# Cross-attention steps that go on in every cell, an earlier norm, and one unit's softmax sums by products with ones

## The chip, the cores and the metric

The kernel runs on one core of one Trainium2 chip. The metric is the device time of one execution in microseconds (us). The kernel before was run three times: 1612.68, 1615.26 and 1616.85 us, median 1615.26. The profiled execution is a fourth one. All arithmetic is in 32-bit floats. In this document PE is the matmul engine (TensorE), PEld its weight loads, DVE is VectorE, ACT is ScalarE, POOL is GpSimd and SP is SyncE.

## The reference

Two transformer blocks run one after the other on x, 2 sequences of 1024 tokens of width 256, with 16 heads of width 16. Each block is self-attention, cross-attention to 64 context rows, and a feed-forward part:

```
x = x + MHA_self(LN(x))                      # 1024 keys per sequence
x = x + MHA_cross(LN(x), context)            # 64 keys per sequence
    s = q @ k.T / 4  (block 2: + mask * -10000)
    a = exp(s - max(s)) / sum(exp(s - max(s)));  out = (a @ v) @ Wo
block 1:  h = LN(x); two of eight experts per token (top-2 of h @ Wr);
          x = x + sum of gate_e * (gelu(h @ W1_e) @ W2_e)
block 2:  x = x + gelu(LN(x) @ W1) @ W2
```

## The kernel before, in words

**Order of work.** Engines execute their queues in the order in which the Python program issues instructions, and that order is written by hand. The program walks over *cells*. A block has 128 of them (`ncell`): 16 groups (2 sequences, 2 halves of queries, 4 groups of four heads) of 8 key blocks. A cell issues, for four heads at once, four score products "b" with the keys on the output partitions (L817), their exponentials (ACT, L823, four to a cell), and for the cell that lies LEAD = 10 ahead four score products "a" (L806) whose row maxima DVE reduces (L813). Every second cell adds the products with the values (L868), copied by ACT (L880 or L877) and added by POOL (L881). Cells 0 to 117 have "a" work (`has_a`); cells 118 to 127 have "b" alone. I call the latter the ten last cells. `maxima[0]` is true where `has_a` is.

**The side work.** Everything else is a generator (a task) in a `Stream`: keys, queries and values of later heads, projections, the cross-attention, and in block 1 the routing ("dispatch"), the search for expert tiles ("find") and the expert slots. A step is what a generator issues until it yields. A yield above zero is a planner's estimate of its PE time. A yield of zero or less holds the task back for at least one cell, more for -3.4 or the like (CELL = 2.9). Each cell adds `max(pace, ...)` to a budget `owed` and calls `stream.step` while it lasts; `pace` is at least RATE = 2.5 us in block 1 and 1.1 us in block 2. In even cells the value product comes first, and if `owed` is below 2.5 the cell ends there with `continue`. At 2.5 per cell this never stops block 1, while in block 2 it does in most even cells. Among the tasks that are able, one with a due time (`last`) goes first, then the one of highest rank. After the last cell, `Stream.rest` issues what is left by rank alone.

**The cross-attention chain.** Each block has four units of 512 tokens, n = 0 to 3 (`cross_tasks`). A unit becomes known when its self-attention output has been projected: `project` (called at cells 39, 71 and 103 for n = 0, 1, 2, and after the cells for n = 3) calls `when_ready`. A unit has three tasks: `norm`, `weigh`, `share`. `norm` waits for the unit before to be weighed. `weigh` makes Q (L1114), then scores (SC, L1148, copied by ACT at L1159), the mask by POOL in block 2 (MA, L1178), the maximum by DVE and its subtraction by POOL (LA, L1168 and L1169), and then goes one of two ways:

- *whole*, if `maxima[0]` is true when it starts: exponentials on ACT (EX, L1185), sums and reciprocals on DVE (L1191, L1192), the division by POOL or DVE (DI, L1193), transposes (TU, L1201, ACT copy L1206) and the value product (PR, L1215). Its steps are laid out in 19 cells (21 in block 2).
- *not whole*: transposes first, exponential on the way out of PSUM (L1208), then `undivided` (value product L1230, sums by products with columns of ones L1240, reciprocal on DVE L1249), and `division` (reciprocals spread by a product, L1255, multiplied by DVE, L1262).

`share` projects the result (L438) and adds it to x (L446). Scores that are made while `maxima[0]` is false get block 2's mask by products with ones on PE (L1139) and their maximum and subtraction by DVE. In the run before, units 0, 1 and 2 of block 1 and 0 and 1 of block 2 are whole; unit 3 of block 1 and units 2 and 3 of block 2 are not.

**What follows a unit.** In block 1, `dispatch_task(n)` waits for `share(n)`, then `find` and `rows`; expert slot 0 needs units 0 and 1, slots 1 to 4 need unit 2, the others unit 3. In block 2, `forward_norm` and `forward_task` follow.

Of the kernel before, what the change touches and what calls it, by code (L numbers as in the profile page):

```python
# [121 lines left out]
class Task:  # L122

    def __init__(self, steps, cost, first=-99, last=None, mark=None, after=(), rank=0):
        self.steps, self.left, self.first = steps, cost, first
        self.soft, self.last = last is None, 9999 if last is None else last
        self.mark, self.after, self.rank = mark, after, rank


class Stream:
# [20 lines left out]
    def step(self, cell):  # L153
        while True:
            able = [t for t in self.tasks if t.first <= cell and self.made.issuperset(t.after)]
            if not able:
                return None
            cost = self.advance(min(able, key=lambda t: (t.last, -t.rank)), cell)
            if cost and cost > 0.0:
                return cost  # L160

    def pace(self, cell):

# [39 lines left out]
def two_blocks(  # L203
# [323 lines left out]
    def self_attention(layer, tail, heads, arrive, extra, when_ready, beside=None):  # L527
# [432 lines left out]
        for cell in range(ncell + 2):  # L960
            now[0] = cell
            ahead = cell + LEAD
            if ahead < ncell and ahead % 16 == 0:
                need_heads(ahead // 8)
            has_a, has_b = ahead < ncell, cell < ncell
            maxima[0] = has_a
            a = [("a", ahead, j) for j in (2, 3, 0, 1)] if has_a else []
            s = [("b", cell, j) for j in range(4)] if has_b else []
            if has_a:
                slot(s[:2] + a[:2])  # L970
                slot(s[2:] + a[2:])
            elif has_b:
                slot(s)
            if ahead % 8 == 7 and has_a:
                h = ahead // 8
                collect(h)
                stream.add(largest(h), 0.75, first=cell + 1, last=cell + 2, mark=("QB", h))
            if (cell + 1) % 8 == 0 and cell + 1 < ncell:
                stream.until(("QB", (cell + 1) // 8))
            for go in later.pop(cell, []):  # L980
                go()
            owed = min(owed, 3.0) + max(stream.pace(cell), 0.0 if has_a else 2.0)
            if cell >= 2 and cell % 2 == 0:
                product([c for c in (cell - 2, cell - 1) if c not in alone])
                if owed < 2.5:
                    continue
            most = 3.0
            while owed > 0.6 and most > 0.0:
                cost = stream.step(cell)
                if cost is None:  # L990
                    break
                owed -= cost
                most -= cost

            if cell % 2 == 1 and most > 2.0 and cell < ncell:
                alone.add(cell - 1)
                product([cell - 1])
# [79 lines left out]
    def cross_tasks(stream, layer, n, pool, first):  # L1077


        att = 2 * layer + 1  # L1080
        w = weights[att]
        b, t0 = n // 2, 4 * n
        name = f"c{layer}{n}"
        held = {}
# [14 lines left out]
        stream.add(  # L1099
            share(w, name, t0, held), 5.0, mark=("cross", n),  # L1100
            after=[("weighed", n)], rank=50,
        )

    def weigh(layer, b, pool, w, name, held):

        att = 2 * layer + 1
        kbd, vbd = kbds[layer], vbds[layer]
# [3 lines left out]
        for g in range(2):  # L1111
            i, p = bank()
            for k in range(2):
                nc.tensor.matmul(  # L1114
                    p,
                    lhsT=w[:, X_Q + k * D + g * P : X_Q + k * D + (g + 1) * P],
                    rhs=xT[:, k, :],
                    start=(k == 0),
                    stop=(k == 1),
                )  # L1120
            nc.scalar.activation(
                q[:, g, :], p, AF.Identity, bias=cols[:, C_Q[att] + g : C_Q[att] + g + 1]
            )
# [149 lines left out]
        if whole:  # L1273

            m = layer
            cells = [[] for _ in range(19 + 2 * m)]
            for k in range(8):
                g, r = divmod(k, 4)
                at = k + (4 + m) * g
                if r % 2 == 0:  # L1280
                    cells[at].append((SC, g, r // 2))
                    cells[at + 7 + m].append((TU, g, r // 2))
                if m:
                    cells[at].append((MA, g, r))
                cells[at + m].append((LA, g, r))
                cells[at + m + 2].append((EX, g, r))
                cells[at + m + 3].append((DI, g, r))
            for g in range(2):
                cells[11 + m + (7 + m) * g].append((PR, g))
            for now in cells:  # L1290
                for step, *args in now:
                    step(*args)
                us = sum(costs.get(step, 0.0) for step, *_ in now)
                if us:
                    yield us
                if now is not cells[-1]:
                    yield 0.0 if maxima[0] else -1.5
            return
        for step, *args, wait in (
            (SC, 0, 0, None),  # L1300
            (SC, 0, 1, -1.0),
# [15 lines left out]
    def share(w, name, first, held):  # L1317

        if held["division"]:
            yield -2.6  # L1320
            held["division"](1)
            yield 0.55
        yield -1.2
        for t0 in range(0, 4, 2):
            yield from project_task(held["ot"], w, first + t0, t0, 2)


    inside = const.tile([P, E], F32, name="inside")
# [869 lines left out]
```

## Time and profile before

| what | us |
|---|---|
| median of three runs | 1615.26 |
| the profiled execution | 1614.59 |
| its span, first to last instruction | 1612.8 |
| cells 0 to 117 of block 1, about | 53.5 to 536 |
| its ten last cells, about | 536 to 566 |
| the rest of block 1, and the experts, about | 566 to 951 |
| cells 0 to 117 of block 2, about | 951 to 1404 |
| its ten last cells, about | 1404 to 1431 |
| the rest of block 2, about | 1431 to 1612.8 |

The span is the time between the first and the last instruction; 1.79 us of the profiled execution lie outside it. The stages are read off from the starts of the exponentials of L823, four to a cell. In a stretch of cells with no side work at all (cells 25 to 27 of block 1) these starts lie 2.92 us apart; with side work a cell takes 3 to 8 us. In the ten last cells they lie 2.4 us apart where nothing else is done.

Where the unit steps ran in the cells before (from the starts of their lines):

| unit | Q (L1114) | first scores | projected (L438) |
|---|---|---|---|
| block 1, n=0 | cell 51 | 52 | 71 to 73 |
| block 1, n=1 | 80 | 81 | 101 to 103 |
| block 1, n=2 | 112 | 113 | 583.7 to 587.3 us, in the rest |
| block 1, n=3 | in the rest | 602.8 us | 639 to 643 us |
| block 2, n=0 | 55 | 61 | 88, 89 |
| block 2, n=1 | 97 | 99 | 123 |
| block 2, n=2 | in the rest | 1444.9 us | 1476.9 us |

### The profile page before, as it was taken

The numbers are of one execution on the slowest core, as the hardware profiler recorded it, in microseconds if no ns is written. First come the engines' busy times: TensorE is split into PE (matmuls) and PEld (weight loads), VectorE is DVE, ScalarE is ACT, GpSimd is POOL, SyncE is SP. The second block draws the span as 40 slices with busy tenths as digits, with TensorE's granted clock in tenths as the row PEclk, the third lists the DMA queues.
The fourth block names the chain that finished last, engine by engine and source line by source line (L and its number), as shares of the span: only waits on it lengthen the run. The fifth ranks groups of instructions, "written<-read, shape, count | busy, mean of one in ns | idle before, by whom it ended". The sixth has DMA issues, their size and how long they took to land. (4 is left out here: it accounts for less than half of the span.)

```text
span 1612.8 us, 27523 instructions
## 1 busy us (share of the span) xinstructions
PE 1560.5 (97%) x10182; PEld 853.7 (53%) x10182; DVE 1013.8 (63%) x2178; ACT 939.3 (58%) x1821; POOL 472.2 (29%) x589
## 2 busy tenths in 40 slices
PE   7999999999999888899999999999999999999998
PEld 3533443443444356688888753344344444446766
DVE  5788776877878856511114458876777878845400
ACT  3488777866867752332333337876777877864321
POOL 2234333433623302311112032411333525511000
PEclk9899999998999999999999999999999999999999
DMA  5236211100100214475656321101110001000000
GB/s 157 113 134 226 81 34 29 34 14 21 41 25 18 67 49 134 153 272 189 203 190 234 92 73 28 35 21 22 34 34 21 22 27 70 22 28 1 14 13 26
DMA packets 55749, 120.98 MB, mean 75 GB/s; under 512 B 12218, under 2 KB 26428, under 8 KB 55228
## 3 DMA queue, kind: packets, MB, share of 16 engines
q1 hardware_dynamic: 51772, 109.02, 21.0%
q0 software_dynamic: 3456, 9.51, 1.6%
q8 instruction: 82, 1.34, 0.3%
q10 hardware_dynamic: 384, 0.66, 0.2%
q14 instruction: 55, 0.45, 0.1%
HBM read 71.64 MB, written 38.88 MB: 69 GB/s over the span
## 5 line engine op out<-in xcount | busy, mean ns | idle before, releaser
L813 DVE TENSOR_REDUCE mx_s<-banks 128x1 f32<-128x512 f32 x1024 | 633.2, 680 | 187.0 <-PE banks L806 182.5
L823 ACT ACTIVATE pt_s<-banks 128x512 f32<-128x512 f32 x1024 | 532.9, 611 | 134.8 <-PE banks L806 107.0
L806 PE MATMUL banks<-KS,QS 16*128 16x512 f32 x2048 | 535.0, 631 | 0.2 <-issue 0.2
L817 PE MATMUL banks<-qb_s,KS 32*128 32x512 f32 x2048 | 516.5, 624 | 7.2 <-DVE qb_s L716 2.3
L881 POOL TENSOR_TENSOR acc_s<-acc_s,part_s 128x512 f32<-128x512 f32 x151 | 191.6, 1269 | 370.3 <-ACT part_s L880 369.2
L817 PEld LDWEIGHTS banks<-qb_s,KS 32*128 32x128 f32 x2048 | 179.3, 187 | 194.5 <-DVE mx_s L813 116.3
L868 PE MATMUL banks<-pt_s,v_s 128*20 128x512 f32 x2048 | 265.8, 604 | 2.6 <-DVE mx_s L813 1.9
L806 PEld LDWEIGHTS banks<-KS,QS 16*128 16x128 f32 x2048 | 199.1, 185 | 64.9 <-issue 29.5
L1731 PE MATMUL banks<-w_slot,h_s 128*128 128x256 f32 x640 | 145.2, 384 | 0.0
L868 PEld LDWEIGHTS banks<-pt_s,v_s 128*20 128x20 f32 x2048 | 42.4, 98 | 191.7 <-ACT pt_s L823 142.9
L1731 PEld LDWEIGHTS banks<-w_slot,h_s 128*128 128x128 f32 x640 | 121.7, 192 | 20.4 <-DVE mx_s L813 1.5
L1740 DVE SCALAR_TENSOR_TENSOR ys<-banks,gate,b 128x256 f32<-128x256 f32 x40 | 19.3, 483 | 172.0 <-PE banks L1731 167.7
L880 ACT COPY part_s<-banks 128x512 f32<-128x512 f32 x166 | 100.3, 605 | 45.8 <-PE banks L868 41.3
L1746 POOL DMA_INDIRECT results<-ys,to x40 | 38.7, 967 | 261.5 <-DVE ys L1740 183.2
L1707 ACT ACTIVATE h_s<-banks,w_slot 128x256 f32<-128x256 f32 x104 | 43.6, 470 | 111.3 <-issue 64.0
L1701 PE MATMUL banks<-xsT,w_slot 128*128 128x256 f32 x416 | 96.2, 383 | 0.9 <-ACT xsT L377 0.9
L1701 PEld LDWEIGHTS banks<-xsT,w_slot 128*128 128x128 f32 x416 | 78.0, 191 | 15.4 <-DVE mx_s L813 2.3
L636 PE MATMUL banks<-xT_s,w_att 128*128 128x512 f32 x128 | 63.9, 635 | 0.5 <-DVE mx_s L813 0.5
L1864 ACT ACTIVATE h_f<-banks,w_ff 128x512 f32<-128x512 f32 x32 | 22.0, 687 | 69.7 <-PE banks L1861 69.7
L1873 PE MATMUL banks<-w_ff,h_f 128*128 128x256 f32 x256 | 57.3, 380 | 0.0
L1707 ACT ACTIVATE h_s<-banks,spare 128x256 f32<-128x256 f32 x56 | 23.5, 470 | 57.3 <-issue 33.4
L1861 PE MATMUL banks<-hT_f,w_ff 128*128 128x512 f32 x128 | 56.8, 594 | 0.0
(282 smaller groups left out, 1666.0 us busy)
## 6 DMA issues: line engine op xcount, KB each, us to landing
w_slot<-in_ff_w_dram SPq DMA_DIRECT2D x40, 576.0 KB
sorted_rows<-fill SPq DMA_DIRECT2D x36, 520.0 KB
w_slot<-in_ff_w_dram SPq DMA_DIRECT2D x26, 514.0 KB
whole<-acc_s SPq DMA_DIRECT2D x30, 256.0 KB
spare<-in_ff_w_dram SPq DMA_DIRECT2D x14, 514.0 KB
xs<-sorted_rows SPq DMA_DIRECT2D x20, 260.0 KB
y<-results SPq DMA_DIRECT2D x16, 256.0 KB
QS<-stq_s SPq DMA_DIRECT2D x124, 32.0 KB
```

What stands on the lines that cost most here:

```text
L636: nc.tensor.matmul(p, lhsT=w[:, at + k * D + pair * P : at + k * D + (pair + 1) * P], rhs=xT[b][:, k, blk * 512 : (blk + 1) * 512], start= ...
L806: nc.tensor.matmul(sc, lhsT=QS[h % 4][r, qc * P : (qc + 1) * P], rhs=K[r, kh * 512 : (kh + 1) * 512], start=True, stop=True,)
L813: return i, lambda: nc.vector.tensor_reduce(mx[h][:, qc, j, kh : kh + 1], sc, AX.X, ALU.max)
L817: nc.tensor.matmul(sc, lhsT=K[r, n * P : (n + 1) * P], rhs=QB[h][r, :], start=True, stop=True)
L823: nc.scalar.activation(pt, sc, AF.Exp, scale=SCALE)
L868: nc.tensor.matmul(o[32 * j : 32 * j + VW, :], lhsT=V[b][:, cell % 8, 4 * g + j, :], rhs=exps.pop((cell, j)), start=(cell == cells[0]), st ...
L880: nc.scalar.copy(part, o)
L881: helper().tensor_tensor(acc[h], acc[h], part, ALU.add)
L1701: nc.tensor.matmul(ph[:, n, :], lhsT=w[:, at : at + P], rhs=xT[:, k, :], start=(k == 0), stop=(k == 1),)
L1707: nc.scalar.activation(h1[:, f, :], ph[:, n, :], AF.Gelu, bias=w[:, W_B1 + f : W_B1 + f + 1])
L1731: nc.tensor.matmul(py, lhsT=h1[:, f, h * P : (h + 1) * P], rhs=w[:, f * D : (f + 1) * D], start=(f == 0), stop=(f == 7),)
L1873: nc.tensor.matmul(py[:, n, :], lhsT=h1[:, f, t * P : (t + 1) * P], rhs=w2[:, f * D : (f + 1) * D], start=(f == 0), stop=(f == 7),)
```

## The change

1. Tasks can be `steady`. In every cell with "a" work a new call `go_on` runs each steady task whose marks are made and whose hold is over, again and again until it has to wait for the next cell. It is called in the even cells too, ahead of `continue`. What it issued is taken from the budget afterwards. The steady tasks are `project`'s, and `norm`, `weigh` and `share` of each unit.
2. `norm` of a unit waits for Q of the unit before (mark `asked`), not for its weights. `weigh` still waits for the unit before to be projected.
3. Unit 2 of block 1 is not whole, even though it starts while `maxima[0]` is true. For that there is a new order of steps, one cell each.
4. `project` and `share` get a `yield 0.0` between their two halves, so that with `go_on` these fall into two cells.

```diff
@@ class Stream
+    def go_on(self, cell):
+        total = 0.0
+        for t in [t for t in self.tasks if t.steady]:
+            while t in self.tasks and t.first <= cell and self.made.issuperset(t.after):
+                total += max(0.0, self.advance(t, cell) or 0.0)
+        return total
@@ project (and share alike)
                 for t0 in range(0, 4, 2):
                     yield from project_task(ot[b, qh], w, b * TB + 4 * qh + t0, t0, 2)
+                    if t0 == 0:
+                        yield 0.0
...
-            stream.add(go(), 4.0, last=now[0] + 4, rank=60, after=after)
+            stream.add(go(), 4.0, last=now[0] + 4, rank=60, after=after, steady=True)
@@ the loop over cells
                 if owed < 2.5:
+                    if has_a:
+                        owed -= stream.go_on(cell)
                     continue
             most = 3.0
+            going = stream.go_on(cell) if has_a else 0.0
+            owed -= going
+            most -= going
             while owed > 0.6 and most > 0.0:
@@ cross_tasks
-        before = [(m, n - 1) for m in ("cross", "weighed")] if n > 0 else ["context"]
-        stream.add(norm(), 2.0, mark=("cnorm", n), after=before[1:], first=first,
-            rank=67 if layer == 0 else 40)
+        before = ("cross", n - 1) if n > 0 else "context"
         stream.add(
-            weigh(layer, b, pool, w, name, held), 17.0,
-            mark=("weighed", n), after=[("cnorm", n), before[0]], rank=30,
+            norm(), 2.0, mark=("cnorm", n), after=[("asked", n - 1)] if n > 0 else [], first=first,
+            rank=67 if layer == 0 else 40, steady=True,
+        )
+        stream.add(
+            weigh(layer, b, pool, w, name, held, lambda: stream.made.add(("asked", n))), 17.0,
+            mark=("weighed", n), after=[("cnorm", n), before], rank=30,
+            steady=True,
         )
@@ weigh
+        asked()
...
-        whole = maxima[0]
+        whole = maxima[0] and (layer, b, held["half"]) != (0, 1, 0)
...
+        if maxima[0]:
+            for now, wait in (
+                (((SC, 0, 0), (LA, 0, 0)), 0.0),
+                (((LA, 0, 1),), 0.0),
+                (((SC, 0, 1), (LA, 0, 2)), 0.0),
+                (((TU, 0, 0), (LA, 0, 3)), 0.0),
+                (((SC, 1, 0), (LA, 1, 0)), 0.0),
+                (((TU, 0, 1), (LA, 1, 1)), 0.0),
+                (((SC, 1, 1), (LA, 1, 2)), 0.0),
+                (((undivided, 0), (LA, 1, 3)), -1.5),
+                (((TU, 1, 0),), None),
+                (((division, 0), (TU, 1, 1)), -1.4),
+                (((undivided, 1),), None),
+            ):
+                for step, *args in now:
+                    step(*args)
+                us = sum(costs.get(step, 0.0) for step, *_ in now)
+                if us:
+                    yield us
+                if maxima[0]:
+                    yield 0.0
+                elif wait is not None:
+                    yield wait
+            return
```

More of the change, by code (lines that the diff above doesn't have):

```diff
@@ L122, with __init__ @@
 class Task:
-    def __init__(self, steps, cost, first=-99, last=None, mark=None, after=(), rank=0):
-        self.steps, self.left, self.first = steps, cost, first
+    def __init__(
+        self, steps, cost, first=-99, last=None, mark=None, after=(), rank=0, steady=False
+    ):
+        self.steps, self.left, self.first, self.steady = steps, cost, first, steady
         self.soft, self.last = last is None, 9999 if last is None else last
@@ L1083, in cross_tasks @@
         name = f"c{layer}{n}"
-        held = {}
+        held = {"half": n % 2}
         def norm():
@@ L1100, in cross_tasks, with weigh @@
             share(w, name, t0, held), 5.0, mark=("cross", n),
-            after=[("weighed", n)], rank=50,
+            after=[("weighed", n)], rank=50, steady=True,
         )
-    def weigh(layer, b, pool, w, name, held):
+    def weigh(layer, b, pool, w, name, held, asked):
         att = 2 * layer + 1
@@ L1298, in weigh @@
             return
+        if maxima[0]:
[11 more added lines that the diff above has]
+                (((undivided, 1),), None),
+            ):
+                for step, *args in now:
[8 more added lines that the diff above has]
+            return
         for step, *args, wait in (
@@ L1325, in share @@
             yield from project_task(held["ot"], w, first + t0, t0, 2)
+            if t0 == 0:
+                yield 0.0
     inside = const.tile([P, E], F32, name="inside")
```

## The prediction

> **What bounds the kernel now.** I read the page's busy time first, then its slices, then a table of stages, then what PE waits for where it idles.
>
> ```profile
> PE 1560.5 (97%) x10182; PEld 853.7 (53%) x10182; DVE 1013.8 (63%) x2178; ACT 939.3 (58%) x1821; POOL 472.2 (29%) x589
> ...
> PE   7999999999999888899999999999999999999998
> ...
> PEclk9899999998999999999999999999999999999999
> ```
>
> PE is the bound nearly everywhere; it misses 52 us of the span. Slices 14 to 17 of 40, about 525 to 685 us, are the one broad hole: the end of block 1's cells and the chain after them. The stages, with busy us of PE, PEld, DVE, ACT and POOL and the granted clock:
>
> ```profile
> 463.00:536.00 73.00, 70.51 (x503) 31.20 (x505) 63.31 (x136) 48.47 (x95) 28.35 (x49) 0.97 0.08 27
> 536.00:566.00 30.00, 27.77 (x212) 10.46 (x204) 22.72 (x60) 26.75 (x54) 5.09 (x5) 0.96 0.16 54
> 1404.00:1431.00 27.00, 26.52 (x199) 10.33 (x196) 12.34 (x38) 23.36 (x48) 2.73 (x2) 1.00 0.03 11
> 566.00:600.00 34.00, 27.74 (x152) 19.15 (x153) 22.52 (x74) 15.67 (x32) 3.16 (x3) 1.00 0.17 59
> 600.00:643.00 43.00, 37.22 (x275) 26.88 (x274) 24.63 (x84) 12.04 (x24) 9.70 (x10) 0.92 0.34 112
> 643.00:690.00 47.00, 40.25 (x187) 33.23 (x186) 26.80 (x120) 17.99 (x35) 18.64 (x21) 0.93 0.50 172
> ```
>
> From 463 to 536 (cells with "a") PE is full and DVE is at 87%. In the ten last cells of either block (536 to 566, 1404 to 1431) ACT is the fullest after PE, at 87 to 89%, and PE's own work there is less than its busy time says: one cell's "b" products take 1.14 us and its share of the value products 0.96 us by the timeline, 21 us for ten, while the cells last 27 to 30. PE waits inside these for exponentials. From 566 to 690 PE idles 18.8 us:
>
> ```profile
> PE banks L370 <- DVE xd_m L1364: 6.5, 1, 6.5
> PE banks L370 <- DVE xn_c L358: 3.6, 2, 1.9
> PE banks L1240 <- issue: 3.1, 6, 1.1
> PE banks L370 <- DMA ctx<-in_ctx_dram: 2.2, 1, 2.2
> PE banks L1437 <- DVE chosen_m L1417: 1.2, 1, 1.2
> PE banks L1201 <- DVE sc_c L1169: 0.9, 2, 0.7
> ```
>
> Columns: us in total, times, longest. Most of it is DVE being late in a normalization or in the routing, with PE's queue standing behind a transpose. These are latencies that the planner's fixed holds did not cover, so having more expert slots at hand does not by itself remove them.
>
> The rows that price the change (busy us, mean ns | idle before):
>
> ```profile
> L1178 POOL TENSOR_TENSOR sc_c<-sc_c,mask_i 128x512 f32<-128x512 f32 x16 | 20.0, 1275 | 13.6 <-ACT sc_c L1159 13.6
> ...
> L1240 PE MATMUL banks<-pt_c,picks 128*32 128x128 f32 x192 | 8.3, 280 | 3.1 <-issue 3.1
> ```
>
> L1178 x16 says that two units of block 2 are whole now. L1240 x192 is six calls of `undivided`, two per unit that is not whole.
>
> **What the skill says.** The Trainium skill, "Perfetto Trace Analysis", Identifying the Most-Contended Engine, says that matmul busy time is a poor measure because matmuls are pipelined. The trace agrees: PE is called 97% busy where, in the last cells, 21 us of work fill 27 to 30. Its page "TensorE: Matmul & The Clock Gate", Part 1, says that the clock is halved after an idle window of about 3.4 us and released by sustained work. Here the granted clock is 0.92 and 0.93 in the two stages with holes; the trace has it halved for 6.8 us each near 641 and 661 us, and 10.2 us near 402. So a hole costs more than its length, but I can't say in advance which ones trigger it.
>
> **Part 1: unit 2 of block 1 by products with ones.** Added on PE: two L1240 groups and two L1255 groups. One group of L1240 took 1.05 us (616.7 to 617.8), one of L1255 1.06. That is 2 x (1.05 + 1.06) = **+4.2 us** of PE (by the page's group rows 2 x (8.3/6 + 6.3/6) = 4.9, with a cold stretch in it; 0 if ACT hides all). Removed: 8 exponentials (L1185, 651 ns) = 5.2 us of ACT, 8 divisions (L1193, 1057 ns) of POOL or DVE. DVE loses 8 sums and reciprocals (670 + 203 ns, 7.0 us) and gains two L1249 (956) and two L1262 (682), 3.3 us. None of these three is the bound while "a" work runs. In the last cells ACT is, and 4 of the exponentials lie there: about 2.6 us of room.
>
> **Part 2: that unit ends earlier.** Its norm can't begin sooner than now: it becomes known at cell 103 or 104. Norm takes 7 cells at one step each, so Q comes at cell 112, as now, where it already takes every cell. The new order needs 11 cells, not 19: seven of them before cell 118, the rest by about cell 122, and `share` by about 125. Now the value product and `share` run at 580 to 587 us. By issue:
> - cells 112 to 117 gain one pair of scores (1.16) and two of transposes (1.06 each): **+3.3 us** of PE at full price;
> - the rest after 566 loses two pairs of transposes (2.1), a value product (1.05) and `share` (3.65): **-6.8**;
> - the ten last cells hold now two pairs of scores, two of transposes, a value product and QB's transposes (6.0 us) beside the 21 us, 27 in 30 us. Then: one pair of scores (1.16), two of transposes (2.1), two `undivided` (2.1 each), two `division` (1.06 each), `share` (3.65) and QB's (0.53), 13.8, so 34.8 us of PE work. ACT falls to about 28. They become PE-bound: **+4.8**. If the budget (3 us a cell) pushes part of `share` behind the cells, the rest grows by what they shrink.
>
> Together 3.3 - 6.8 + 4.8 = **+1.3**: the 4.2 us of added work, less 3 us of PE time that ACT wastes now. Bounds 0 and +4.9.
>
> **Part 3: the rest of block 1.** The routing of unit 2 now interleaves on DVE with the norm of unit 3 (586 to 599 us), and its `find` with that unit's scores (619 to 637). Both move to about 565 to 600, partly ahead of unit 3's start. The 3.6 us before xn_c and 1.2 before chosen_m should shrink; the 6.5 us before xd_m of unit 3 have a different cause (DVE's small operations run slowly beside POOL's fills of KS and QS) and stay. Bounds 0 to -10 (all but the xd_m and DMA waits); I take **-4**. Weight loads on SP and eight scatters on POOL's queue (L1474, 989 ns each) come some 25 us earlier with it. No other work is queued behind them on SP in that stretch but the loads themselves.
>
> **Part 4: block 1's first two units.** `go_on` takes unit 0 from cell 51 to 48 and its end from 73 to 68, so its routing begins at 69, four cells sooner than unit 1's norm and scores. These two pile up now: cells 80 to 90 last 56.9 us, while 11 x 2.93 plus the PE steps in them (Q 3.7, router 1.9, three pairs of scores 3.5, transposes 3.2, queries 1.85, others 0.9) come to 47.3. The surplus of 9.6 us is DVE late with row maxima, and the half clock near 402. I take a third of it, **-3**; bounds +3 (another pile-up, since `find` for two units then falls into cells with "a" work) and -8.
>
> **Part 5: block 2.** At one step a cell unit 0 runs at cells 48 to 70 instead of 55 to 89, unit 1 at 80 to 102 instead of 97 to 123, and unit 2 starts Q at 112, while `maxima[0]` is true, so it turns **whole**. The condition exempts block 1 alone. PE loses two `undivided`-sums and two `division`, 4.2 us, and the mask products of its first two pairs of scores: a pair with mask takes 1.75 to 2.05 us (1444.9 to 1448.4 for two), without 1.16, so 2 x 0.7 = 1.4. Sum **-5.6 us** in a block that PE bounds. Against it: five of its exponentials (0.65 each) fall into the ten last cells, where ACT takes 27 us already, +3.3, of which PE work moved there hides a part: **+2**. And POOL: a score's maximum on DVE (0.67), its subtraction (1.05) and the next score's mask (1.28) follow each other, and come now at every cell: 3.0 us, with POOL's adds (1.27 each second cell) 3.6, while a cell with half a pair of scores is 2.93 + 0.58 = 3.5. That is even. Price 0 to 0.65 x 20 masked scores = 13; I take **+2**, as POOL's few steps each cell already ran at 1241 to 1256 us and PE showed no gap there.
>
> **Edits at no cost.** The wait on `asked` is met long before (Q of unit 0 at cell 48, norm of unit 1 at 73), so nothing stands behind it. The `yield 0.0` between halves changes places alone, 1.9 us of PE on either side.
>
> **Sum.** 1.3 - 4 - 3 - 5.6 + 2 + 2 = -7.3 us. The profiled execution has 1614.59, which gives 1607.3. It lies 0.67 below the median shown, inside the runs' 4 us of spread, so I leave it at **1607.3**.
>
> **Rivals.** *All holes close* (0.12): parts 3 to 5 reach their good ends, -10, -8 and no POOL price: 1.3 - 10 - 8 - 5.6 + 2 = -20.3, 1594.3. For it: the surplus is visible in the trace. Against: PE's queue is in order, and more supply does not shorten DVE's chains.
> *A wash* (0.22): the earlier routing and `find` pile up elsewhere (part 4 at +3, part 3 at 0): 1.3 + 3 - 5.6 + 2 + 2 = +2.7, or with part 5's POOL at 0, +0.7: about 1616. For it: cells 112 to 117 are already 8 us over their PE work.
> *Slower: POOL's mask chain holds DVE* (0.23). DVE is in order, so a maximum that waits for its mask holds the row maxima of "a" behind it, these hold banks, and PE stops. At 0.65 us for each of 20 masked scores it costs 13, with part 4 at 0 and part 3 at -2: 1.3 - 2 - 5.6 + 2 + 13 = +8.7, 1623.3. It decides where a cell is shorter than POOL's 3.6 us: any cell without scores or another PE step. For it: L1178 has 1275 ns and the order is fixed. Against: in the present run DVE never waits for POOL in those cells.
> *The change doesn't do what it says* where the steps were already one per cell: true for units 1 and 2 of block 1, and counted so.
>
> **Numbers.** Forecast 0.43, by itself 1602 to 1611. About 0.3% (4.8 us) is what a measurement of this kernel can tell from no change. Faster 0.43 + 0.12 = 0.55; same 0.22; slower 0.23. The range, 1595 to 1623, leaves out about half of the first rival and half of the last, 0.17.
>
> **What would show it.** Right: L1178 at x20 and L1139 at x96, L1185 still x40, L1240 still x192; no "xn_c" wait after 566 us; cells 80 to 90 of block 1 under 53 us; last cells of block 1 near 35 us and of block 2 near 29. Wrong: DVE waiting for POOL in L1168 of block 2; PE idle from 566 to 690 still at 18 us or more; new half-clock stretches in the cells. If unit 2 of block 2 were not whole, 5.6 us of the gain would be missing.

## The result, and the profile after

The kernel after takes 1626.83 us (median of 5 runs, 1623.88 to 1632.69); the kernel before had 1615.26 in the 5 runs beside it (1612.68 to 1617.32). The ratio is 1.0074, 95% interval 1.0048 to 1.0100: the change makes the kernel **slower by 0.7%**, where 1607.3 was forecast. The profiled execution took 1623.88 us with a span of 1622.1, so it lies at the low end of its runs; the one before, 1614.59 with 1612.8.

The page's first view, busy time, and its slices show nothing of that at first sight:

```profile
PE 1575.6 (97%) x10150; PEld 852.6 (53%) x10150; DVE 1006.7 (62%) x2157; ACT 939.7 (58%) x1824; POOL 485.8 (30%) x615
...
PE   7999999999999999999999999999899999999998
...
PEclk9899999998999999999999999999899999999999
```

The hole of slices 14 to 17 is closed, and yet PE is busy 15 us longer with 32 products fewer. The record calls PE busy at half clock too, as the stretches of cell 112 below show. A new notch stands in slice 29 of 40, in both rows: about 1160 us, in block 2.

The stages, read from the starts of L836's exponentials (the L823 of before; every line of the kernel after lies 11 to 49 further down), in us. The ten last cells are counted to the start of cell 127's:

| stage | before | after | difference |
|---|---|---|---|
| up to cell 40 of block 1 | 199.2 | 197.5 | -1.7 |
| block 1, cells 40 to 117 | 336.7 | 359.2 | **+22.5** |
| block 1, ten last cells | 29.8 | 34.4 | +4.6 |
| rest of block 1, and the experts | 385.2 | 364.6 | **-20.6** |
| block 2, cells 0 to 117 | 453.5 | 480.9 | **+27.4** |
| block 2, ten last cells | 26.7 | 29.5 | +2.8 |
| rest of block 2 | 181.7 | 156.0 | -25.7 |
| sum | 1612.8 | 1622.1 | +9.3 |

Most of block 2's two large numbers is unit 2 moving from the rest into the cells. What is stall and what is moved work I estimated with a price per cell: 2.93 us (2.39 in the last cells), plus the PE steps found in the cell at their durations at full clock. In block 1's cells PE's side work grew by about 3 us, so some 19 of the 22.5 are stalls; in block 2's cells 40 to 117 time grew by 27.7 and side work by about 14, so some 14 are stalls, 8 to 10 of them in one cell.

The stretches that answer to those shown of before: cells 104 to 117 of block 1, its last cells, block 2's last cells, and three pieces of the rest (us, then busy us of PE, PEld, DVE, ACT, POOL, then the granted clock, DMA share and GB/s):

```profile
483.00:556.50 73.50, 69.56 (x453) 29.42 (x446) 54.28 (x123) 46.44 (x89) 29.69 (x38) 0.93 0.09 30
556.50:591.00 34.50, 34.38 (x312) 15.15 (x308) 17.49 (x46) 24.45 (x48) 1.04 (x1) 1.00 0.13 40
1436.60:1466.00 29.40, 29.40 (x262) 12.57 (x260) 18.26 (x31) 27.93 (x57) 3.52 (x3) 1.00 0.03 11
591.00:622.00 31.00, 28.58 (x153) 19.30 (x146) 22.80 (x108) 14.39 (x30) 7.58 (x9) 0.94 0.26 90
622.00:660.00 38.00, 36.12 (x290) 27.88 (x289) 20.16 (x52) 17.52 (x34) 6.50 (x7) 1.00 0.59 215
660.00:705.00 45.00, 40.60 (x191) 32.74 (x190) 24.43 (x107) 13.82 (x28) 18.55 (x22) 1.00 0.43 139
```

The last cells are PE-bound now, 34.38 of 34.50. Of 114 us in the rest PE idles 8.7, not 18.8, and the clock is full in two of the three pieces. What PE waits for there, from 591 to 705 us (us in total, times, longest):

```profile
PE banks L381 <- DVE xd_m L1413: 3.3, 2, 2.1
PE banks L1780 <- ACT h_s L1756: 2.9, 1, 2.9
PE banks L1224 <- DVE sc_c L1192: 0.9, 2, 0.6
PE banks L1487 <- DVE before_m L1479: 0.6, 2, 0.3
```

No xn_c is left in it. The groups that price the change (busy us, mean ns | idle before):

```profile
L1208 ACT ACTIVATE sc_c<-sc_c 128x512 f32<-128x512 f32 x40 | 26.2, 656 | 0.0
L1201 POOL TENSOR_TENSOR sc_c<-sc_c,mask_i 128x512 f32<-128x512 f32 x20 | 25.1, 1274 | 18.5 <-ACT sc_c L1182 18.5
...
L1263 PE MATMUL banks<-pt_c,picks 128*32 128x128 f32 x192 | 6.3, 273 | 0.0
```

These are the forecast counts: x20 masks by POOL, x40 exponentials, x192 products with ones.

**Two places.** The first is in block 1: cell 80, 375.8 to 388.3 us, and cell 112, 520.4 to 532.5, with cell 48, 233.1 to 241.7, to compare (same columns as above):

```profile
375.80:388.30 12.50, 12.50 (x63) 4.85 (x62) 3.91 (x10) 5.04 (x9) 1.26 (x1) 0.73 0.06 22
520.40:532.50 12.10, 12.10 (x61) 4.51 (x61) 3.50 (x10) 5.17 (x11) 1.26 (x1) 0.74 0.06 22
233.10:241.70 8.60, 8.60 (x59) 3.81 (x56) 2.79 (x5) 4.95 (x9) 1.26 (x1) 1.00 0.09 33
```

The three cells hold the same: a value product, all of Q (L1135) and the first scores (L1171), in that order, since `go_on` runs a unit until it must wait, and between Q's halves and the scores nothing makes it wait. I call this the burst. In the quiet cell 48 it makes a cell of 8.6 us. Cells 80 and 112 last 12.5 and 12.1 us, against 7.4 and 7.9 before, where cell 80 had half of Q and cell 112 all of it, and the scores came a cell later. (In e1 and e3 below, which issue the same in block 1, the two last 10.3 to 10.9.) DVE works only 3.5 to 3.9 us of each. What DVE waits for, from 375 to 390 us of the kernel after, and from 518 to 535:

```profile
DVE mx_c L1191 <- ACT sc_c L1182: 8.3, 1, 8.3
...
DVE mx_c L1191 <- ACT sc_c L1182: 7.5, 1, 7.5
```

The same in the kernel before, from 365 to 385 us and from 505 to 530:

```profile
DVE mx_s L813 <- PE banks L806: 3.9, 1, 3.9
DVE mx_c L1168 <- ACT sc_c L1159: 3.7, 1, 3.7
...
DVE mx_s L813 <- PE banks L806: 2.6, 1, 2.6
```

DVE stands in front of the first cross-attention maximum while PE works off the burst. At cell 112 that is a longer wait than before. At cell 80 DVE waited as much before, in two pieces.

The half clock in these cells is not made by their bursts, for it begins ahead of them. From the cell before on:

```profile
370.40:375.80 5.40, 3.54 (x28) 1.73 (x22) 5.26 (x12) 3.36 (x8) 2.47 (x2) 1.00 0.00 2
376.40:381.80 5.40, 5.40 (x24) 0.92 (x20) 2.98 (x7) 1.53 (x3) 0.00 (x0) 0.50 0.00 0
511.00:519.80 8.80, 6.13 (x39) 3.64 (x41) 8.63 (x18) 4.57 (x9) 2.49 (x2) 1.00 0.01 3
519.80:526.60 6.80, 6.80 (x29) 1.72 (x24) 3.66 (x12) 2.37 (x5) 0.00 (x0) 0.50 0.00 0
526.60:532.50 5.90, 5.90 (x39) 3.19 (x38) 0.36 (x1) 2.94 (x6) 1.26 (x1) 1.00 0.13 46
```

Ahead of both cells DVE is full (5.26 of 5.40 us and 8.63 of 8.80) and PE is not: it waits for row maxima, at most 1.9 us at a time. Then comes half clock, and only then Q, which starts at 381.9 us in cell 80 and at 526.7, at full clock again, in cell 112. Besides row maxima DVE has the routing of the unit before there and the norm of this one. Unit 0's routing has its transposes in cell 75 and its small DVE operations in cells 78 and 79, and unit 1's norm lies in cells 73 to 79. In the kernel before these operations came in cells 82 to 84, behind that norm.

The other place is cell 54 of block 2: 12.6 us, before 5.3. PE, 1160 to 1180 us:

```profile
PE banks L819 <- DMA QS<-stq_s: 4.5, 1, 4.5
PE banks L830 <- DVE qb_s L727: 0.9, 1, 0.9
```

The keys and queries of the next heads are not there. Their 16 DMAs (L663, on SP, about 0.65 us each) are issued at 1158.5 to 1168.9 us, while cells 52 to 54 run; before, at 1121.9 to 1142.1, in cells 45 to 51.

### The profile page after: what moved, and what is told of

It reads as the page before. It is cut to its first block, busy times and chain, and to the rows that moved or that the text cites. A ratio compares the mean times of both kernels' runs of the same rounds, so it can differ in the third digit from the quotient of the medians.

```text
span 1622.1 us, 27470 instructions
## 1 busy us (share of the span) xinstructions
PE 1575.6 (97%) x10150; PEld 852.6 (53%) x10150; DVE 1006.7 (62%) x2157; ACT 939.7 (58%) x1824; POOL 485.8 (30%) x615
## 5 line engine op out<-in xcount | busy, mean ns | idle before, releaser
L836 ACT ACTIVATE pt_s<-banks 128x512 f32<-128x512 f32 x1024 | 533.9, 608 | 154.1 <-PE banks L819 111.0
L819 PE MATMUL banks<-KS,QS 16*128 16x512 f32 x2048 | 548.3, 633 | 5.8 <-DMA QS<-stq_s 4.5
L881 PE MATMUL banks<-pt_s,v_s 128*20 128x512 f32 x2048 | 271.4, 613 | 0.6 <-ACT pt_s L836 0.5
L1750 PEld LDWEIGHTS banks<-xsT,w_slot 128*128 128x128 f32 x416 | 77.4, 190 | 14.9 <-DVE mx_s L826 2.3
L1192 POOL TENSOR_TENSOR sc_c<-sc_c,mx_c 128x512 f32<-128x512 f32 x42 | 43.8, 1044 | 62.2 <-DVE mx_c L1191 56.4
```

The costliest lines, as they stand in the source:

```text
L819: nc.tensor.matmul(sc, lhsT=QS[h % 4][r, qc * P : (qc + 1) * P], rhs=K[r, kh * 512 : (kh + 1) * 512], start=True, stop=True,)
L836: nc.scalar.activation(pt, sc, AF.Exp, scale=SCALE)
L881: nc.tensor.matmul(o[32 * j : 32 * j + VW, :], lhsT=V[b][:, cell % 8, 4 * g + j, :], rhs=exps.pop((cell, j)), start=(cell == cells[0]), st ...
L1750: nc.tensor.matmul(ph[:, n, :], lhsT=w[:, at : at + P], rhs=xT[:, k, :], start=(k == 0), stop=(k == 1),)
```

## The experiments

Ratios are to the kernel before, run in between. Its medians on the chips of the experiments were 1609.1 to 1610.8 us. Stage times are from each profiled execution. Executions differ by several us, with half-clock stretches in other places: e1, e3 and the kernel after issue the same in block 1 and have 749.6, 752.2 and 758.2 us for it from cell 40 on (356.6, 359.1 and 359.2 in the cells). So a ratio, or a stage that differs by more than that, counts here, not a span alone. The kernel after itself was not run on these chips; its ratio is the 1.0074 above.

**e1: go_on not charged in block 2.** In both places of the loop:

```diff
-            owed -= going
+            owed -= going * (layer == 0)
```

> In block 2 what go_on issues is no longer taken from the budget; all else as in the changed kernel. Theory (the charge starves the keys' and queries' steps that issue DMAs, 16 of them are then forced at cell 54 and PE waits): the 12.6 us of cell 54 of block 2 fall to about 4.3 and the half-clock stretch at 1165 us goes, so the time is about 8 us below the changed kernel, near 1618. Rival (that cell is long for another reason, POOL's division and adds): cell 54 stays above 10 us and the time near 1626.

1618.58 us, ratio 1.0043 (1.0029 to 1.0058). Cell 54 takes 4.5 us: the charge starved the DMAs. But cells 105 to 109 grew from 17.9 to 23.7 us, with 13.7 us of half clock from 1382.7, and block 2 is 665.0 instead of 666.4. In the profiled execution one stall was traded for another. A forward norm starts there a cell sooner, in cell 107, beside unit 2's norm; that this is the reason is not shown.

**e2, e3, e5: go_on in block 2 alone, in block 1 alone, in neither.** The four `steady=True` become:

```diff
-            steady=True
+            steady=layer == 1        # e2;  e3: layer == 0;  e5: False
```

> The tasks are steady in block 2 alone; block 1 paces its unit steps by the budget as before, its third unit still by products with ones. Theory (in block 1 the cells lose 19 us to DVE pile-ups of routing and norm with half clock, and the rest after them gets back about 14 of it): cells 40 to 117 of block 1 fall from 359 to about 340 us, the rest grows by 10 to 15, and the time is 4 to 7 us below the changed kernel, near 1621. Rival (block 1's loss comes from the sums by products, not from the pacing): cells 40 to 117 stay above 352 us and the time near 1627.

> The tasks are steady in block 1 alone; block 2 as before the change. Theory (block 2 is a net loss of 4 to 5 us, made of 14 us of stalls against 9 us of work and idle saved): near 1622. Rival (earlier steps in block 2 are a gain, the loss is all in block 1): 1630 or more.

> No task is steady, so go_on issues nothing: the norm's wait for Q, the third unit by products with ones and the two halves stay. Theory (stages add up, and go_on is a loss in both blocks): block 1 as in the run with steady tasks in block 2 alone, block 2 as in the run with steady tasks in block 1 alone, so a span of 1597.8 - 668.7 + 657.3 = 1586 us, 22 to 24 us below the kernel before. Rival (part of block 1's gain hangs on block 2's or the reverse): 1595 or more.

e2: 1600.63, ratio 0.9943 (0.9927 to 0.9959). Block 1's cells fall to 338.1 as expected, but the rest does *not* grow back, 359.3. e3: 1612.81, ratio 1.0021 (1.0010 to 1.0031), where about 1622 was expected, a ratio of 1.0042: block 2 without go_on has 657.3. e5: 1591.66, ratio **0.9887 (0.9871 to 0.9904)**, with e11 the fastest version found. Its stretches in block 1, last cells and three pieces of the rest:

```profile
535.40:569.80 34.40, 33.14 (x313) 16.10 (x316) 20.17 (x46) 25.91 (x51) 4.75 (x5) 1.00 0.14 44
569.80:600.00 30.20, 26.86 (x146) 17.58 (x139) 20.98 (x96) 17.23 (x33) 2.35 (x3) 1.00 0.21 70
600.00:643.00 43.00, 42.05 (x318) 33.69 (x317) 28.67 (x83) 17.94 (x36) 17.13 (x20) 1.00 0.60 207
643.00:690.00 47.00, 46.70 (x223) 39.09 (x222) 19.34 (x94) 16.42 (x34) 14.60 (x15) 1.00 0.58 188
```

PE idles 4.6 us of the last three and the clock is full throughout. From block 1's cell 40 on, e5 has 730.0 us for block 1 and 660.7 for block 2; before 751.7 and 661.9; after 758.2 and 666.4. So the change is two: everything but `go_on` gains 22.9 us of span, and `go_on` costs 32.2: 28.2 in block 1 and 5.7 in block 2, less 1.7 ahead of cell 40, where it issues nothing. With the two other profiles of block 1 the 28.2 are 19.6 (e1) and 22.2 (e3). The ratios say the same without profiles: against e5, `go_on` costs 0.6% in block 2 alone (e2), 1.3% in block 1 alone (e3) and 1.9% in both (the kernel after).

**e4: the third unit left whole.**

```diff
-        whole = maxima[0] and (layer, b, held["half"]) != (0, 1, 0)
+        whole = maxima[0]
```

> The exception for block 1's third unit is taken out, so it is whole in 19 cells; go_on and the norm's wait stay. Theory (the products with ones cost 4.2 us of PE but let the unit end before the last cell, which closes some 10 us of PE's idle time after the cells): the last cells shorten by 3 to 4 us, the idle time from 591 to 705 us grows from 9 to 15 or more, and the time is within 4 us of the changed kernel, rather above, 1627 to 1631. Rival (the products with ones are the loss): 1620 or less.

1636.15, ratio 1.0173 (1.0149 to 1.0197). Last cells 29.5, rest 375.9. Against the changed kernel the rest takes 11.3 us more, the last cells 4.9 less and the cells ahead of them 2.2 more: the products with ones are worth far more than the 0 to 4 us expected. Only a part of it is holes: from cell 127 to the end of the rest PE idles 14.8 us here and 11.1 in the kernel after, and half clock takes 6.8 us, not 3.4. The other part, as an estimate, is the 6.8 us of work that part 2 of the prediction had moved out of the rest and that lies in it again.

**e6: the third unit by products with ones, nothing else.** `steady=False`, no `yield 0.0` between halves, and in `cross_tasks`

```diff
-            norm(), 2.0, mark=("cnorm", n), after=[("asked", n - 1)] if n > 0 else [], first=first,
+            norm(), 2.0, mark=("cnorm", n), after=[("weighed", n - 1)] if n > 0 else [], first=first,
```

> The kernel before with one part of the change alone, the third unit of block 1 by products with ones. Theory: block 1 gains 17 us by it (PE's idle time after the cells closes), block 2 stays as before, so a span near 1592 us, 16 to 20 us below the kernel before. Rival (the gain needs the norm's earlier start): within 5 us of the kernel before.

1595.61, ratio 0.9903 (0.9885 to 0.9920). Block 1's cells 334.7, last 36.2, rest 359.8; in the rest PE idles 5.9 us, not 21.0 as before. That single part is nearly the whole of e5's gain. The two intervals overlap, so what the earlier norm and the halves add is not settled.

**e7: the first unit's routing held until unit 1 has its Q.**

```diff
-                    + ([("found", n)] if n > 1 else []),
+                    + ([("found", n)] if n > 1 else []) + ([("asked", 1)] if n == 0 else []),
```

> The changed kernel, with the routing of block 1's unit 0 held until unit 1 has made Q. Theory (routing and norm pile up on DVE): the time of cells 75 to 89 beyond PE's own work falls from 15.7 to about 8 us and the time by 5 to 8; cells 105 to 119 stay. Rival (the unit steps themselves, one cell each, cost the stalls): cells 75 to 89 keep 13 us or more of it, the time within 3 us of the changed kernel.

1623.60, ratio 1.0080 (1.0064 to 1.0097). Cells 75 to 84 fell from 54.4 to 40.9 us, cells 85 to 99 rose from 61.3 to 77.8. The pile-up went where the routing went, and no time was gained. Cell 80, which still holds the whole burst, is as short as the quiet cell 48:

```profile
366.10:374.70 8.60, 8.60 (x59) 3.79 (x56) 2.81 (x5) 4.95 (x10) 1.26 (x1) 1.00 0.09 31
```

**e8: block 1's first scores a cell after Q.**

```diff
         asked()
+        if layer == 0 and maxima[0]:
+            yield 0.0
```

> The changed kernel, with block 1's first scores of a unit one cell after Q instead of in the same one. Theory (the long cells 80 and 112 are long from the half clock and the pile-up ahead of them): the two cells together with the next ones keep their time, within 2 us. Rival (one cell with 4.9 us of side work is itself the cause): cells 80 to 81 and 112 to 113 lose 3 us or more each and the time 6 or more.

1617.91, ratio 1.0050 (1.0035 to 1.0066). Cells 80, 81 and 112, 113 shrank by 2.9 and 1.9 us, but cells 75 to 84 and 110 to 114 together stayed within 1 us, and e1 and e3, without this edit, have 14.7 and 14.9 us in cells 80 and 81 and 13.7 in 112 and 113, where e8 has 13.7 and 13.6; block 1's cells have 356.8. That decides nothing about the burst: all of Q, 3.7 us of the 4.9 of Q and scores, was still in one cell.

**e9: without POOL's additions in unit norms.** The output bias of block 1's self-attention is not added (`add_bias(t0, 4, bias_out[1])` in `norm`), so part of the computation is left out.

> The changed kernel without block 1's add of the output bias to x in the norm of a unit (the sum bias_out[1] is left out: eight POOL additions of 1.27 us). Theory (in the pile-ups DVE's small two-input operations of the routing, 0.19 us each elsewhere, take 0.8 to 1.1 us beside these POOL additions): the time of cells 75 to 84 and 110 to 114 beyond PE's own work falls by 2 to 4 us each and the total by 3 to 8. Rival (it is the number of DVE operations, not POOL's additions): under 1 us each.

1616.18, ratio 1.0052 (1.0035 to 1.0069). Block 1's cells 350.8; cells 75 to 84 have 49.3 and 110 to 114 25.9 us, and the half-clock stretches at 376 and 520 us are gone, while one of 6.8 us stands at 413.6. So by the stages the additions were part of it; the time does not settle it, since the intervals of the ratios overlap. In the trace DVE's small operations are stretched beside POOL's additions (last section); that they act by this is not shown. DVE operations of under 0.3 us in block 1's cells 45 to 117 take, beyond the median of their line, about 9 us before, 9 after, 5 in e5, 5 here and 3 in e12: the amount does not tell after from before.

**e10: unit 1 of block 1 by products with ones as well, on e5.**

```diff
-        whole = maxima[0] and (layer, b, held["half"]) != (0, 1, 0)
+        whole = maxima[0] and (layer, b, held["half"]) not in ((0, 1, 0), (0, 0, 1))
```

> The kernel without go_on, and block 1's unit 1 by products with ones too. Theory (unit 2 gains by its place, since it ends ahead of the chain after the cells; a unit in the middle only pays 4.2 us of PE): 0 to 4 us above the kernel without go_on. Rival (the products with ones gain anywhere, as they free DVE, ACT and POOL): 4 us or more below it.

1600.58, ratio 0.9939 (0.9919 to 0.9959): against e5 the cells go from 336.2 to 346.1, and the rest stays (360.0, 359.4). So products with ones are no cheaper by themselves: they gain at unit 2, which stands ahead of the rest, and not at unit 1.

**e11: e2 with a budget that go_on cannot drive below zero.**

```diff
-            owed -= going
+            owed = max(0.0, owed - going) if going else owed
```

> Steady tasks in block 2 alone, and what go_on issues may take the budget to zero but not below. Theory (the stall of cell 54 comes from a negative budget; go_on has no gain of its own left in block 2): cell 54 under 6 us, block 2 near 661 us instead of 668.7, the time equal to the kernel without go_on within 4 us. Rival (go_on in block 2 gains once nothing starves): 5 us or more below the kernel without go_on.

1591.46, ratio 0.9892 (0.9874 to 0.9910). Cell 54 takes 7.1 us; block 2 660.3, e5 without go_on 660.7. Once it starves nobody, go_on in block 2 is worth nothing either way.

**e12: half of Q a cell in block 1.** The changed kernel with one more break:

```diff
             yield 1.72
+            if layer == 0 and maxima[0]:
+                yield 0.0
         asked()
```

> The changed kernel with one more break in block 1 alone: after each half of Q (L1135) the unit waits for the next cell, so that cells 48, 80 and 112 hold half of Q each instead of all of Q and the first scores. Theory A, burst: in cell 80 the value product, all of Q and the first scores stand in PE's queue one after the other, DVE gets no 'a' product for 8.3 us, and a DVE that is nearly full cannot make it up. Then cells 75 to 84 (54.4 us) fall to about 47 and cells 110 to 114 (32.6) to about 26, block 1's cells from 359 to about 346, and the time to about 1602 where the kernel before has 1610 to 1615 (ratio 0.998 to 1.001). Theory B, the routing of unit 0 beside unit 1's norm and POOL's additions makes the whole pile-up, wherever Q stands: block 1's cells stay at 355 or more, ratio 1.004 or more. Half a score more or less per cell (e8) gave 2.4 us, and theory B expects about that here.

1619.60, ratio 1.0077 (1.0054 to 1.0100). The stages are what the burst theory said: cells 75 to 84 44.8 us, cells 110 to 114 26.6, block 1's cells 343.5. But the edit does two things. With Q in two cells unit 0 ends two cells later, and so does its routing begin: its product L1426 (L1428 here) goes from cell 76 to 78 and its small DVE operations to cell 80, behind unit 1's norm. Of the 9.6 us that cells 75 to 84 lose, 4.9 lie in cells 75 to 79, ahead of Q. So e12 does not part the burst from the routing. The half clock in cell 80 is gone, the one in cell 112 is still there (6.8 us from 510.0). DVE in cells 80 to 86 (369 to 400 us; lines below L1147 lie 2 further down here and in e13):

```profile
DVE mx_c L1193 <- ACT sc_c L1184: 1.9, 1, 1.9
DVE mx_s L826 <- PE banks L819: 1.6, 2, 0.9
```

The time did not follow. Units advance more slowly, so unit 2 ends at cell 126 instead of 124: the last cells take 39.8 (34.4 after), and its projection is cut by the end of the cells. The rest takes 366.6, with PE idle 4.6 us before context rows that are loaded late. Block 1 from cell 40 on is 749.9, no less than e1's 749.6.

**e13: the burst put into e5.** In block 1 Q's halves yield nothing, and the first score's step is charged 3.44 us more:

```diff
-            yield 1.72
+            if layer == 1 or not maxima[0]:
+                yield 1.72
```

> The kernel of e5 (no go_on) with the burst put in: in block 1 both halves of Q and the first scores of a unit are one step, so they stand in one cell, charged 3.44 us more. Theory A: 4 to 5 us each for units 1 and 2 (unit 0's cell is quiet and costs about 1), block 1's cells from 336 to 343 to 347, span from 1590 to about 1599, ratio 0.992 to 0.996. Theory B: the routing is where it was, so at most 2 us, ratio 0.987 to 0.990.

1602.35 (12 runs), ratio 0.9958 (0.9947 to 0.9970), where e5 has 0.9887 (0.9871 to 0.9904). Block 1's cells take 345.1 (e5 336.2), cell 80 10.1 and cell 112 14.6; the intervals are apart. DVE's wait, 363 to 376 us of this kernel:

```profile
DVE mx_c L1193 <- ACT sc_c L1184: 6.2, 1, 6.2
```

In all that is no more than in e5, where DVE waits 3.9 and 3.7 us from 365 to 382. This is the burst alone, with no go_on at all: 0.7%. Where it costs is another matter. Unit 1's burst has cost nothing by cell 112, and all 8.9 us come in cells 112 to 117. There too the half clock begins first, at 506.4 us, and Q at 513.0, and the routing of unit 1 lies a cell earlier than in e5 (L1490 in cell 112; in e5 L1486 in 113).

**e14: both faults mended, in both blocks.** e12's break without `layer == 0`, and e11's budget.

> The changed kernel with go_on mended in both ways known by then: half of Q a cell in both blocks, and a budget that go_on cannot drive below zero in either. Theory A: block 1's cells about 346 or below, block 2 about 660 as in e11, together 359 + 666 - 346 - 660 = 19 us less than the changed kernel, ratio about 0.996. Theory B: block 1's cells stay at 355 or more, ratio 1.000 or more. Neither expects it below the kernel without go_on (0.989).

1618.55, ratio 1.0070 (1.0044 to 1.0097). Block 1's cells 343.2, but last 39.8 and rest 366.6 as in e12; block 2 666.4, not 660: cell 54 takes 7.7 us, and 10.2 us of half clock stand at 1296.5. So the clamp gives block 2 back in e11 and not here, where Q also comes in two cells. Mending both leaves `go_on` a loss.

**Where block 1's cells fall behind.** How many us more than e5 each kernel has taken, from the start of cell 40 to the start of the cell named:

| | 76 | 81 | 94 | 111 | 118 |
|---|---|---|---|---|---|
| after | 5.3 | 17.4 | 8.5 | 10.9 | 23.0 |
| e1 | 5.3 | 16.5 | 7.6 | 10.0 | 20.4 |
| e3 | 5.3 | 15.7 | 10.1 | 12.5 | 22.9 |
| e7, routing held | 2.7 | 4.2 | 8.2 | 12.5 | 22.9 |
| e12, half of Q a cell | 2.6 | 4.7 | 2.7 | 2.6 | 7.4 |
| e13, e5 with the burst | 0.0 | 2.7 | -1.3 | -1.3 | 8.9 |

The long cell 80 is mostly work and waiting that e5 has a little later: by cell 94 the kernel after has 8.9 of its 12.1 us back. What stays is the 5.3 ahead of cell 76 and the 10 to 12 of cells 111 to 117, unit 2's place, which e13 shows as well and e12 has down to 4.8. The clock is a small part of the 23.0. In cells 40 to 117 half clock takes 20.5 us after, 17.1 before and 13.7 in e5; at half speed the 6.8 between after and e5 are worth at most 3.4 us, an estimate from these figures.

## Why the prediction was wrong, step by step

The sign came from two steps. The parts that counted operations were right; those that said what a moved step meets were not. (The half-clock stretches that I put near 402, 641 and 661 us lie at 391.5, 630.4 and 650.9 in time from the span's start.)

**Part 1, +4.2 us of PE.** Right: a group of L1263 takes 6.3 / 6 = 1.05 us.

**Part 2, last cells 34.8 us, together +1.3.** The last cells are 34.4, with the steps in them that were laid out.

**Part 3, -4 in the rest of block 1, next to -6.8 of moved work.** The mechanism was right and the size far off: the rest lost 20.6 us, and 25.8 in e5, where 10.8 were forecast. PE's idle time fell from 18.8 to 8.7 (4.6 in e5), and the half clock at 630 and 651 us, each 6.8 us long, went with it; one of 3.4 us came at 598. With the 6.8 us of moved work that adds up, as an estimate: 6.8, 10.1 of idle time and half of 10.2 for the clock make 22.0. I held that xd_m's 6.5 us had another cause and would stay; it is 3.3 after and not among e5's. Of the 6.5, the operations that were slow beside POOL's fills (L328, L332 and L335, 1.37, 0.94 and 0.94 us) make up no more than half. I also charged no clock to the holes, though I had written that a hole costs more than its length. The rival *all holes close*, with -10 here, was nearer. Its sum, 1594.3, is near e5's profiled execution, 1591.66, by luck: e5 has nearly all of its gain in the end of block 1, and part 4 and block 2, to which the rival gave 11.6 us, have 0.5 and 1.2.

**Part 4, -3 from an earlier first unit.** The first failed step, and its sign was wrong: block 1's cells take 359.2 with go_on (e1 356.6, e3 359.1) and 336.2 without (e5), and before 336.7. The prediction let the routing begin at 69, four cells sooner than unit 1's norm and scores, and took that for parting them. It does begin in cell 68. But it lasts to cell 82, so its small DVE operations moved from behind unit 1's norm onto it. And I read "one step a cell" where the code says "until it has to wait": Q's two halves and the first scores are three steps with no wait between them. Putting that burst in alone costs 8.9 us of cells and 0.7% of time (e13); taking the routing away from unit 1's norm, with the burst left in, brings cells 75 to 84 from 54.4 to 40.9 us, but not the sum of the cells (e7). Taking both apart brings cells 75 to 84 to 44.8 us, before's 44.7, and the cells to 343.5 (e12). The test that I set, cells 80 to 90 under 53 us, failed (56.2), and new half-clock stretches in the cells, named as a sign against me, came at 366, 376, 520 and 547 us, where before had two, at 391 and 531. The bound of +3 for another pile-up named the kind of loss, and about a seventh of its size.

**Part 5, block 2, -5.6 + 2 + 2.** The counts are right, and so is ACT's price (last cells +2.8). POOL's mask chain cost nothing that shows: in block 2's cells from 40 on DVE waits for L1201 for 0.7 us in all. What it missed is cell 54, +7.3 us. I listed the effects on PE, ACT and POOL, and for *edits at no cost* looked only at what stands behind the new wait. The queue that mattered was SP's: the charge to `owed` takes the turn of tasks whose steps cost nothing by the planner but issue DMAs. Block 2 as a whole became 4.5 us longer instead of 1.6 shorter; with the charge clamped e11 has 660.3, as without go_on (e5, 660.7).

**The rival that ended slower** had 1623.3 by a mask chain that holds DVE. The figure is near the result, 1626.8, and the mechanism is not in the trace (the 0.7 us of part 5), so the nearness is luck.

**The clock.** The Trainium skill, "TensorE: Matmul & The Clock Gate", Part 1, speaks of an idle window of about 3.4 us ahead of the half clock. Here PE was given half clock at 376.4 and 519.8 us after gaps of at most 1.9 and 1.6 us in its record, with PE busy 36.6 of 39 us around the first (355 to 394). For this kernel the measurement decides: stretches in which PE was partly idle were enough.

**What stays open.** That `go_on` is the loss is shown. In block 2 the way is shown too, the charge that goes below zero (e1 for cell 54, e11 for the block); why e14, with the same clamp, still has 666.4 there is open. In block 1 the way is shown in part. The burst costs 8.9 us of cells by itself, at unit 2 alone, and the routing on top of the norm makes cells 75 to 84 long, but no run parts the two at unit 2. Nor does any run explain all of the 5.3 us ahead of cell 76. e12 and e14, with shorter cells, have the time mostly taken back in the last cells and the rest: against e5, e12 still has 7.3 us more in the cells, 5.4 in the last cells and 7.2 in the rest. That its steps come at a fixed pace and displace the other tasks at the end of the cells is argued from their place, not shown. Whether POOL's additions act by DVE's stretched operations alone was not tried separately.

## What to carry to other kernels

Ask of a scheduling change not only when each step now comes but how many land back to back in one slot, and what else is still running there. A value product, all of Q and the first scores in a row (1.9 + 3.7 + 1.2 us of PE at full clock) made a cell of 8.6 us where DVE had little else to do, and of 10.1 to 14.6 us beside the routing. A task that starts sooner is not therefore out of its neighbour's way: the routing, begun in cell 68 instead of 74, came to have its small operations on the norm that they had followed. Check the order in time before calling a burst the cause of a slow clock; here the half clock came first. A budget that may go negative starves steps that cost nothing by its count, and those may issue the DMAs that everything waits for (cell 54: 12.6 us instead of 5.3). Try the parts of a bundled change one by one: here one part is worth -1.0%, and another turned the whole into +0.7%.

## What the runs showed of the hardware

- The three cells with the same products took 8.6 us at full clock (cell 48) and 12.1 and 12.5 at a granted clock of 0.74 and 0.73 (cells 112 and 80), PE being called busy for all of it.
- A DVE comparison of 128x32 elements (L1450) took 0.19 us as a rule and 1.03 to 1.08 in three of eight cases of the kernel after, each of them beside a POOL addition of 128x512 (1.26 to 1.28 us). The Trainium skill, "SBUF — State Buffer", Who interferes with whom, says that DVE and POOL exclude each other at a shared port; the trace fits for these, which read two tiles, and prices such a meeting at 0.8 to 0.9 us. It says as well that a DVE operation with one input outside the faster modes does not contend. The one-input multiplication and addition L1458, 0.17 us as a rule, took 1.29 once (371.6 us), beside such an addition; in which mode it ran no trace shows.
- Half-clock stretches that ended inside the span lasted 3.4, 6.8, 10.2, 13.7 or 17.1 us in all traces (17.1 in e6 and e7), multiples of 3.4.
